# Macaron block on one core: how weight loads are cut, which engine adds the gate sums, where attention keeps its transposed tokens, and in what order blocks and attentions run

## The chip, the cores and the metric

The kernel runs on one core of a Trainium2 chip. The metric is device time in microseconds (us) for the whole program, lower is better; the time of a kernel is the median of its runs.

## The reference, cut to what matters

Eight sequences of 512 tokens with 512 features pass through a feed-forward part, an attention and a second feed-forward part, all in float32. The two feed-forward parts use the same weights.

```
x = x + 0.5 * ffn(layernorm(x), w_gate, w_up, w_down)
x = x + attn(layernorm(x), W_q, W_k, W_v, W_o)
x = x + 0.5 * ffn(layernorm(x), w_gate, w_up, w_down)

ffn:  h = silu(x @ w_gate) * (x @ w_up)            # hidden 2048
      keep, of each 4 neighbours in h, the 2 largest magnitudes
      return h @ w_down
attn: Q (16 heads of 32), K and V (4 heads, tiled), rotary positions on Q and K
      softmax(Q K^T / sqrt(32)) V, then @ W_o
```

## The kernel before, in words

**Blocks.** A block (b, i) is feed-forward part i (0 before, 1 after the attention) of sequence b: 16 blocks, run one after the other in the order of the list `blocks` (lines 90 to 93). Each block has four chunks of 512 hidden features, and each chunk two pairs. A pair is one Strassen-like product of seven half-size products (`woven`, lines 613 to 686), named by the quarter of the weight that they use: Q11, S1, S2, S4, S3, Q12, Q22 in this order. Their results are collected in `x`, `v` and `z` in PSUM and in `row` and `corner` in SBUF; VectorE (DVE) adds them (`add`, line 638), ScalarE copies or VectorE does (`copied`, lines 242 and 244). A product of eight matmul records of 256 columns takes 1.73 us of TensorE (PE). Then the two of four are kept by some 16 short VectorE instructions for each half of a chunk (`keep_two_of_four`, lines 393 to 452), while GpSimd (POOL) makes the sums `e` (lines 446 to 451). After every second chunk come seven products with `w_down` (`products`, line 532), whose results VectorE adds to the tokens (line 565).

**Gate sums.** S1 to S4 are sums of the quarters Q11, Q12, Q21, Q22 of the gate and up weights. The opening block (0, 0) loads four quarters of each pair and makes the sums of the pair after the current one when three groups of the current pair are through (`combine_gu`, line 688): VectorE adds (line 693, on the queue `for_later`, the last in rank), and SP stores each sum to DRAM (line 694). Every later block loads the sums (line 116). The sums for `w_down` are made in the opening block too: `combine_down` (line 492) loads a 1 MB chunk `raw` (line 496), GpSimd makes five sums of 1 x 512 per partition (line 505), and SP stores them (line 506); it runs for two chunks in each of two calls.

**Attention.** `attention(b)` (line 772) runs beside the blocks. It loads W_k, W_q, W_v into one tile (lines 775 to 778) and the rotary tables `cs` (line 780), then normalises and transposes the tokens (`layernorm_t`, line 278), projects, takes the maxima of the scores (VectorE, line 843), turns them into pieces in bfloat16 (lines 851 to 854), makes the exponentials (ScalarE, line 879), multiplies with V (line 887), sums the exponentials on VectorE (line 895), divides, and multiplies with W_o (line 972), which it loads as one DMA after the projections (line 830).

**Buffers.** The transposed tokens `xT` of blocks and of attentions come from the same pool of two (`xtp`, line 317); the list `in_xT` holds those in use, and the last step of a norm's scaling isn't passed while two are (line 349). The pool `p_slots` has two buffers of 8 KB per partition: `raw`, then in each attention `cs`, the first exponentials that become `total`, and the other exponentials `p`. PSUM has three single banks, taken in turn (`Bank`, line 225).

**Order of the work.** The program is written out by a planner in Python that keeps a clock for PE, VectorE and ScalarE. The main loop (line 1047) goes through the groups of the blocks; n counts groups, a half-size product of a pair counts 0.5, and a block is WIDTH = 42 units of n. After each group it may let each side stage (a norm for the next block, an attention, `combine_down`) take one step, if the step is due by n and what it waits for is ready by the planner's clock. A side has a first and a last n (lines 1003 to 1017) and its steps are spread between them in proportion to WEIGHTS; an attention has 57 steps with weights of 44.1 in all, the first 19 (norm and projections) at 0.5. Attention's stretch before is computed by lines 1007 to 1017: it starts no sooner than the last one ended, is moved to the start of a block if it would start more than 17 units into one, and gets an equal share of what is left or 1.4 blocks, whichever is longer. The norm for a block stands from 15 to 2 units ahead of it. VectorE's work waits in three queues (`urgent`, `put_off`, `for_later`) and in the steps of `keep_two_of_four`, and is written out when the planner's clock lets it fit (`fill`, line 374). All DMAs are issued by SP, in program order; a DMA that waits for its buffer or its source holds the ones behind it.

Of the kernel before, what the change touches and what calls it, by code (L numbers as in the profile page):

```python
# [11 lines left out]
FP = mybir.dt.float32  # L12
BF = mybir.dt.bfloat16
AF = mybir.ActivationFunctionType
ALU = mybir.AluOpType
# [11 lines left out]
def macaron_block(  # L27
# [59 lines left out]

    Q11, Q12, Q22, Q21, S1, S2, S3, S4 = range(8)
    gu_sums = [dram.tile([P, 4, 2, ND // 2, P], FP, name=f"gu_{i}") for i in range(2 * NCH)]
    blocks = [(0, 0), (1, 0)]  # L90
    for b in range(2, B):
        blocks += [(b, 0), (b - 2, 1)]
    blocks += [(B - 2, 1), (B - 1, 1)]
    coming = deque()
    for block in blocks:
        for i in range(2 * NCH):
# [181 lines left out]
    def layernorm_t(got, tag, src=None, xb=None):  # L278
# [33 lines left out]

        def turn(t):
            if t == 0:
                assert len(in_xT) < 2
                in_xT.append(got)
                got["xT"] = xtp.tile([P, ND, S], FP, tag="xT", name="xT")
            xT = got["xT"]
            tr = transposed([xn[t][:, c * P : (c + 1) * P] for c in range(ND)])
            nc.scalar.copy(xT[:, :, t * P : (t + 1) * P], tr.tile)  # L320
            tr.free(end=takes("act", 0.6, pe_heard()))
# [11 lines left out]
        if xb is None:  # L333
            there = at["pe"] + 10.0
            yield lambda: there
            found = [soon(0.9, partial(moments, t)) for t in (0, 1)]
            yield now
            found += [soon(0.9, partial(moments, t)) for t in (2, 3)]
            yield partial(when, found[:2])
            ensure(found[:2])  # L340
            scales((0, 1))
            yield partial(when, found)
            ensure(found)
            scales((2, 3))
            yield by_scalar
            for t in range(NT):
                normalise(t)
                end = at["act"]
                yield by_scalar if t < NT - 1 else lambda: max(end, by_scalar()) if len(in_xT) < 2 else None
            for t in range(NT):  # L350
                turn(t)
                yield by_scalar if t < NT - 1 else now
            if tag == "xf":
                sums()
        else:

            function(AF.Sqrt)
            for t in range(NT + 1):
                if t < NT:
                    moments(t)  # L360
                    va = rs[:, 0, t : t + 1]
                    nc.vector.tensor_scalar(va, mv[:, t, 1:2], EPS, None, ALU.add)
                    nc.scalar.activation(va, va, AF.Sqrt)
                if t:
                    i = t - 1
                    nc.vector.reciprocal(rs[:, 1, i : i + 1], rs[:, 0, i : i + 1])
                    nc.vector.tensor_scalar(
                        xn[i], xb[:, i, :], mv[:, i, 0:1], rs[:, 1, i : i + 1], ALU.subtract, ALU.mult
                    )
                    turn(i)  # L370
            function(AF.Silu)
            sums()
# [119 lines left out]
    def combine_down(g):  # L492

        for c in range(2 * g, 2 * g + 2):
            raw = p_slots.tile([P, 4, D], FP, "raw")
            nc.sync.dma_start(out=raw, in_=w_down[c])
            there = at["pe"] + 12.0
            yield lambda: there
            yield now
            quarter = {f"{i + 1}{j + 1}": raw[:, i::2, j * HD2 : (j + 1) * HD2] for i in range(2) for j in range(2)}  # L500
            sums = wa_slots.tile([P, 6, 2, HD2], FP, "sums")

            for i, name in enumerate(SUMS):
                op = ALU.add if name[2] == "+" else ALU.subtract
                nc.gpsimd.tensor_tensor(sums[:, i], quarter[name[:2]], quarter[name[3:]], op)
                nc.sync.dma_start(out=combined[g, name][:, c % 2 * 2 : c % 2 * 2 + 2, :], in_=sums[:, i])
            yield now
        done_down.add(g)
# [13 lines left out]
    def ffn(b, final, last):  # L522
# [165 lines left out]
        def combine_gu(i):  # L688

            w = [quarters[(b, final), i, q] for q in range(8)]  # L690

            def one(j, a, b, op):
                nc.vector.tensor_tensor(w[j], a, b, op)
                nc.sync.dma_start(out=gu_sums[i][:, j - S1], in_=w[j])

            gu_made[i] = [
                later(0.62, partial(one, j, w[a], w[b], op), at["pe"], for_later)
                for j, a, b, op in (
                    (S1, Q21, Q22, ALU.add),
                    (S2, S1, Q11, ALU.subtract),  # L700
                    (S3, Q11, Q21, ALU.subtract),
                    (S4, Q12, S2, ALU.subtract),
                )
            ]

        opens = (b, final) == blocks[0]
        hs, last_one = [], []
# [64 lines left out]
    def attention(b):  # L772
        ensure(written[b, 0])
        wa = wa_slots.tile([P, ND, D + 2 * KV], FP, "wqkv")
        for src, col in ((w_k, D), (w_q, 0), (w_v, D + KV)):
            nc.sync.dma_start(
                out=wa[:, :, col : col + src.shape[1]], in_=src.rearrange("(c p) n -> p c n", p=P)
            )
        cs = p_slots.tile([P, 4, S], FP, "cs")
        nc.sync.dma_start(out=cs[:, :2, :], in_=rope.rearrange("a p s -> p a s"))  # L780
        got = {}
        yield from layernorm_t(got, "xa", tokens[b][1])
        xT = got["xT"]
        qT = qkvp.tile([P, ND, S], FP, tag="qT", name="qT")
        kT = qkvp.tile([P, S], FP, tag="kT", name="kT")
# [2 lines left out]
        def projected(dst, col, scale):  # L788
# [13 lines left out]
            ps.free([read])  # L802
            soon(0.65, partial(nc.vector.scalar_tensor_tensor, sw, sw, scale, cs[:, 1, :], ALU.mult, ALU.mult))
            made = soon(0.65, partial(nc.vector.tensor_tensor, dst, dst, sw, ALU.add))
            return [p_slots.used(w_slots.used(made))]

        of_k = projected(kT, D, 1.0)
        yield now
# [14 lines left out]
                )  # L823
        multiplied(3.57)
        fill()
        in_xT.remove(got)
        nc.scalar.copy(v, vps.tile)
        vps.free(end=takes("act", 0.6, pe_heard()))
        wo = wa_slots.tile([P, ND, D + 2 * KV], FP, "wo")
        nc.sync.dma_start(out=wo[:, :, :D], in_=w_o.rearrange("(c p) n -> p c n", p=P))  # L830
        yield partial(when, of_k + of_q[0])

        def scores(c, t, nm):
# [86 lines left out]
        ensure(of_k + of_q[0])  # L920
        for t in range(NT):
            found = scores(0, t, nm)
            yield partial(when, found)
        pieces = in_pieces(nm)
        yield partial(when, pieces)
# [74 lines left out]
        return WIDTH * blocks.index((b, i))  # L1000


    sides = [(11, 18, 6, partial(combine_down, 0), None, None), (22, 32, 6, partial(combine_down, 1), None, None)]
    for b, i in blocks[1:]:
        stage = partial(layernorm_t, normed[b, i], "xf", tokens[b][2 * i])
        sides.append((place(b, i) - 15, place(b, i) - 2, NORM, stage, ("attention", b) if i else None, None))
    before = 0
    for b in range(B):

        left = place(B - 1, 1) - 13 - before  # L1010
        first = max(before, place(b, 0) + WIDTH + 16)
        if first % WIDTH > 17:
            first += WIDTH - first % WIDTH
        last = min(place(b, 1) - 13, max(before + left / (B - b), first + 1.4 * WIDTH))
        assert last - first > ATTENTION * 0.8
        sides.append((first, last, ATTENTION, partial(attention, b), ("attention", b - 1) if b else None, ("attention", b)))
        before = last
    sides.sort(key=lambda s: s[0])

    for _ in layernorm_t(normed[0, 0], "xf", xb=xs[0, 0]):  # L1020
# [98 lines left out]
```

## Time and profile before

| what | us |
|---|---|
| median of 3 runs (lowest, highest) | 3226.03 (3221.42, 3229.11) |
| the profiled execution's own time | 3222.35 |
| its span in the trace | 3220.5 |
| mean granted clock of PE | 0.999 |
| first matmul record, last product's end | 6.2, about 3216.5 |
| gate sums on VectorE (line 693), 32 instructions | 26.4 |
| `w_down` sums on GpSimd (line 505), 20 instructions | 27.3 |
| sums `e` and `h` on GpSimd (lines 446 to 451), 310 instructions | 424.8 |
| `w_q` and `w_o`, 1 MB each, issue to landing, median | 9.0, 5.2 |
| `raw`, 1 MB, issue to landing, median | 7.2 |

The span is the profiled execution from its first to its last instruction. A line of a stretch gives from:to, its length, and for each engine the busy time with the number of instructions (PE, PEld, the weight loads, DVE, ACT, POOL), then the granted clock of PE as a share, the busy share of the DMA engines and the GB/s. A line of the waits gives the waiting engine, tile and line, what it waited for, the time in total, the number of waits and the longest. A line of the timeline gives the start, the length, the engine, line and operation, the tile written and those read, the number of instructions merged, and in brackets the idle time before with what ended it.

### The profile page before, as it was taken

What the parts mean: (1) busy time and instruction counts of PE and PEld (TensorE: products, weight loads), DVE (VectorE), ACT (ScalarE), POOL (GpSimd) and SP (SyncE); (2) the same over time, 40 slices, a digit from 0 to 9 for tenths busy, and PEclk for the clock granted to TensorE, in tenths of its full rate; (3) what the DMA queues carried; (4) which work ended last, traced back from release to release, by engine and by line L of the source; (5) the groups of instructions that cost most, each with busy time, mean ns of one, the idle gap of its engine ahead of it and who ended that gap; (6) DMA issues with size and microseconds to landing.
All of it is one profiled execution on the core that took longest, in us unless ns stands there. A gap on an engine that the chain in (4) does not pass through costs nothing.

```text
span 3220.5 us, 43674 instructions
## 1 busy us (share of the span) xinstructions
PE 3180.1 (99%) x15880; PEld 2320.9 (72%) x15880; DVE 2281.7 (71%) x4869; ACT 1182.0 (37%) x1669; POOL 608.1 (19%) x888
## 2 busy tenths in 40 slices
PE   8999999999999999999999999999999999999999
PEld 6886668766776677767776668666776668666886
DVE  6867875678577775887578766678577775787554
ACT  2222552145324441354314532145324542255211
POOL 2422011211221112111121112111120122201120
PEclk9999999999999999999999999999999999999999
DMA  7762345433533434434543345333533446234451
GB/s 241 245 215 95 113 145 171 138 116 111 194 111 122 157 121 160 138 125 150 166 140 122 119 155 197 120 108 113 202 102 121 156 124 214 95 112 147 152 172 46
DMA packets 249285, 463.21 MB, mean 144 GB/s; under 512 B 24432, under 2 KB 64368, under 8 KB 248304
## 3 DMA queue, kind: packets, MB, share of 16 engines
q1 hardware_dynamic: 249072, 460.42, 43.3%
q8 instruction: 127, 2.08, 0.3%
q14 instruction: 86, 0.70, 0.1%
HBM read 421.53 MB, written 38.80 MB: 143 GB/s over the span
## 4 chain that ended last, share of the span: by engine, by line
PE 94%; DVE 3%; DMA 1%; ACT 1%; issue 0%; SPq 0%; DVEq 0%; ACTq 0%
PE x L624 26%; PE y L552 23%; PE v L624 13%; PE z L624 6%; PE proj L792 4%; PE sc L838 4%; PE st L871 4%; PE ops L887 4%; PE y L972 3%; PE tr L262 2%; PE gu L599 1%; PE den L903 1%; PE vps L817 1%; PE y L582 1%; PE st L876 1%; DMA xn<-x 1%
## 5 line engine op out<-in xcount | busy, mean ns | idle before, releaser
L624 PE MATMUL x<-ts,w 128*128 128x256 f32 x3000 | 720.2, 383 | 6.2 <-DVE corner L638 5.9
L624 PEld LDWEIGHTS x<-ts,w 128*128 128x128 f32 x3000 | 561.0, 190 | 151.4 <-issue 48.1
L552 PE MATMUL y<-wd,h 128*128 128x256 f32 x1984 | 455.2, 383 | 9.0 <-DVE h L440 6.4
L552 PEld LDWEIGHTS y<-wd,h 128*128 128x128 f32 x1984 | 372.8, 190 | 97.2 <-issue 28.8
L446 POOL TENSOR_TENSOR e<-h 128x512 f32<-128x512 f32 x62 | 96.6, 1559 | 1495.7 <-DVE h L440 1364.5
L164 DVE TENSOR_REDUCE nm<-sc 128x1 f32<-128x512 f32 x512 | 320.8, 683 | 63.5 <-PE sc L838 62.0
L565 DVE SCALAR_TENSOR_TENSOR x<-y,x 128x512 f32<-128x512 f32 x372 | 242.2, 686 | 135.6 <-PE y L552 133.8
L552 PE MATMUL y<-wd,e 128*128 128x256 f32 x1488 | 335.3, 380 | 1.0 <-PE den L903 1.0
L552 PEld LDWEIGHTS y<-wd,e 128*128 128x128 f32 x1488 | 281.3, 190 | 53.5 <-issue 11.0
L164 DVE TENSOR_TENSOR total<-total,p 128x512 f32<-128x512 f32 x384 | 266.2, 734 | 58.2 <-ACT p L879 58.2
L879 ACT ACTIVATE p<-st 128x2048 f32<-128x2048 f32 x96 | 179.6, 1870 | 283.2 <-PE st L876 191.3
L254 ACT ACT_TABLE_LOAD x206 | 264.3, 1283 | 4.4 <-PEq L1108 0.7
L673 ACT ACTIVATE h<-x 128x256 f32<-128x256 f32 x125 | 47.5, 380 | 592.8 <-PE x L624 573.1
L242 ACT COPY row<-x 128x512 f32<-128x512 f32 x210 | 122.9, 585 | 383.2 <-PE x L624 382.3
L624 PE MATMUL v<-ts,w 128*128 128x256 f32 x1000 | 238.8, 382 | 3.5 <-ACT xT L320 2.9
L624 PE MATMUL x<-xT,w 128*128 128x256 f32 x1000 | 239.8, 383 | 0.0
L624 PE MATMUL z<-xT,w 128*128 128x256 f32 x1000 | 239.4, 382 | 0.0
L624 PE MATMUL v<-xT,w 128*128 128x256 f32 x1000 | 239.0, 382 | 0.4 <-ACT corner L242 0.4
L624 PEld LDWEIGHTS x<-xT,w 128*128 128x128 f32 x1000 | 186.4, 190 | 50.8 <-issue 24.0
L624 PEld LDWEIGHTS v<-ts,w 128*128 128x128 f32 x1000 | 187.6, 190 | 46.9 <-issue 15.1
L624 PEld LDWEIGHTS z<-xT,w 128*128 128x128 f32 x1000 | 186.4, 190 | 48.2 <-issue 20.9
L624 PEld LDWEIGHTS v<-xT,w 128*128 128x128 f32 x1000 | 187.3, 190 | 45.5 <-issue 11.8
(109 smaller groups left out, 4114.0 us busy)
## 6 DMA issues: line engine op xcount, KB each, us to landing
w<-gu SPq DMA_DIRECT2D x472, 256.0 KB, 3.3
w<-in_w_gu SPq DMA_DIRECT2D x394, 256.0 KB, 3.3
wd<-wd SPq DMA_DIRECT2D x155, 512.0 KB, 3.8
wd<-in_w_down SPq DMA_DIRECT2D x124, 256.0 KB, 4.9
x<-x SPq DMA_DIRECT2D x64, 256.0 KB, 2.6
xn<-x SPq DMA_DIRECT2D x64, 256.0 KB, 6.9
x<-in_x SPq DMA_DIRECT2D x32, 256.0 KB, 3.4
gu<-w SPq DMA_DIRECT2D x32, 256.0 KB, 2.6
```

The lines of the kernel that those rows point to most:

```text
L164: self.does()
L242: nc.scalar.copy(dst, src)
L254: nc.scalar.activation(dummy[:, 1:2], dummy[:, 0:1], f)
L552: nc.tensor.matmul(out=y.tile[:, t, :], lhsT=part[:, t * P : (t + 1) * P], rhs=operands[i][:, n, :], start=(n == 0), stop=(n == 3),)
L565: nc.vector.scalar_tensor_tensor(to, y.tile, 0.5 * sign, to, ALU.mult, ALU.add)
L624: nc.tensor.matmul(out=bank.tile[:, m, :], lhsT=lhs[:, m, k, :], rhs=rhs[:, k, :], start=(first and m == 0 and k == 0), stop=(k == 1), ski ...
L792: nc.tensor.matmul(out=ps.tile, lhsT=wa[:, k, col : col + P], rhs=xT[:, k, :], start=(k == 0), stop=(k == ND - 1))
L838: nc.tensor.matmul(out=sc[:, kv, :], lhsT=qT[rows, c, t * P : (t + 1) * P], rhs=kT[rows, :], start=True, stop=True)
L871: nc.tensor.matmul(out=st[:, kv, :], lhsT=kT[rows, t * P : (t + 1) * P], rhs=qT[rows, c, :], start=True, stop=False)
L879: nc.scalar.activation(p, st, AF.Exp)
L887: nc.tensor.matmul(out=ops[rows, :], lhsT=v[:, t, rows], rhs=p[:, kv, :], start=(t == 0), stop=(t == NT - 1))
L972: nc.tensor.matmul(out=y.tile, lhsT=qT[:, k, t * P : (t + 1) * P], rhs=wo[:, k, :D], start=(k == 0), stop=(k == ND - 1))
```

## The change

Five things are done together.

1. The gate sums of the opening block are added by GpSimd, at the place where they were put on the queue before, and each is stored by SP right behind it.
2. Loads of 1 MB are cut into DMAs of 256 KB, each issued at a step of its side stage: `raw`, W_q, W_o; the rotary tables in two. In the attention the tokens are now loaded first, and W_k, W_v, the tables and W_q follow one at each of the first eight steps of the norm. `combine_down` has ten steps instead of six, and stretches from 10 to 19 and from 22 to 34.
3. Attention's `xT` is taken from `p_slots`; only the blocks' `xT` count in `in_xT`.
4. The order of blocks becomes, with b.i for block (b, i): 0.0, 1.0, 2.0, 3.0, 0.1, 4.0, 1.1, 2.1, 5.0, 6.0, 3.1, 7.0, 4.1, 5.1, 6.1, 7.1. Before it was 0.0, 1.0, 2.0, 0.1, 3.0, 1.1, 4.0, 2.1, 5.0, 3.1, 6.0, 4.1, 7.0, 5.1, 6.1, 7.1.
5. The attentions get equal stretches of n, one behind the other, from 58 to 617.

```diff
-    blocks = [(0, 0), (1, 0)]
-    for b in range(2, B):
-        blocks += [(b, 0), (b - 2, 1)]
-    blocks += [(B - 2, 1), (B - 1, 1)]
+    first_of = {0: 0, 1: 1, 2: 2, 3: 3, 5: 4, 8: 5, 9: 6, 11: 7}
+    second_of = {4: 0, 6: 1, 7: 2, 10: 3, 12: 4, 13: 5, 14: 6, 15: 7}
+    blocks = [(first_of[i], 0) if i in first_of else (second_of[i], 1) for i in range(2 * B)]
...
-                assert len(in_xT) < 2
-                in_xT.append(got)
-                got["xT"] = xtp.tile([P, ND, S], FP, tag="xT", name="xT")
+                if tag == "xf":
+                    assert len(in_xT) < 2
+                    in_xT.append(got)
+                    got["xT"] = xtp.tile([P, ND, S], FP, tag="xT", name="xT")
+                else:
+                    got["xT"] = p_slots.tile([P, ND, S], FP, "xT")
...
-            nc.sync.dma_start(out=raw, in_=w_down[c])
-            there = at["pe"] + 12.0
-            yield lambda: there
-            yield now
+            for r in range(4):
+                nc.sync.dma_start(out=raw[:, r], in_=w_down[c][:, r])
+                there = at["pe"] + 5.0
+                yield now if r < 3 else lambda: there
...
-            def one(j, a, b, op):
-                nc.vector.tensor_tensor(w[j], a, b, op)
+            for j, one, two, op in (
+                (S1, Q21, Q22, ALU.add),
+                (S2, S1, Q11, ALU.subtract),
+                (S3, Q11, Q21, ALU.subtract),
+                (S4, Q12, S2, ALU.subtract),
+            ):
+                nc.gpsimd.tensor_tensor(w[j], w[one], w[two], op)
                 nc.sync.dma_start(out=gu_sums[i][:, j - S1], in_=w[j])
-            gu_made[i] = [
-                later(0.62, partial(one, j, w[a], w[b], op), at["pe"], for_later)
...
-            ]
+            gu_made[i] = [Done(at["pe"] + 8.0)]
...
-        for src, col in ((w_k, D), (w_q, 0), (w_v, D + KV)):
-            nc.sync.dma_start(
-                out=wa[:, :, col : col + src.shape[1]], in_=src.rearrange("(c p) n -> p c n", p=P)
-            )
         cs = p_slots.tile([P, 4, S], FP, "cs")
-        nc.sync.dma_start(out=cs[:, :2, :], in_=rope.rearrange("a p s -> p a s"))
+        loads = deque()
+        for src, col in ((w_k, D), (w_v, D + KV)):
+            loads.append((wa[:, :, col : col + KV], src.rearrange("(c p) n -> p c n", p=P)))
+        for i in range(2):
+            loads.append((cs[:, i], rope[i]))
+        for k in range(ND):
+            loads.append((wa[:, k, :D], w_q[k * P : (k + 1) * P, :]))
         got = {}
-        yield from layernorm_t(got, "xa", tokens[b][1])
+        for ready in layernorm_t(got, "xa", tokens[b][1]):
+            if loads:
+                dst, src = loads.popleft()
+                nc.sync.dma_start(out=dst, in_=src)
+            yield ready
...
-        nc.sync.dma_start(out=wo[:, :, :D], in_=w_o.rearrange("(c p) n -> p c n", p=P))
...
         for t in range(NT):
             found = scores(0, t, nm)
+            nc.sync.dma_start(out=wo[:, t, :D], in_=w_o[t * P : (t + 1) * P, :])
...
-    sides = [(11, 18, 6, partial(combine_down, 0), None, None), (22, 32, 6, partial(combine_down, 1), None, None)]
+    sides = [(10, 19, 10, partial(combine_down, 0), None, None), (22, 34, 10, partial(combine_down, 1), None, None)]
...
-        left = place(B - 1, 1) - 13 - before
-        first = max(before, place(b, 0) + WIDTH + 16)
-        if first % WIDTH > 17:
-            first += WIDTH - first % WIDTH
-        last = min(place(b, 1) - 13, max(before + left / (B - b), first + 1.4 * WIDTH))
+    bounds = [WIDTH + 16 + b * (place(B - 1, 1) - 13 - WIDTH - 16) / B for b in range(B + 1)]
+    for b, (first, last) in enumerate(zip(bounds, bounds[1:])):
```

The smaller edits left out let a norm for an attention pass without counting in `in_xT` (line 349), and record the last use of `cs` one buffer back in `p_slots` (line 805).

## The prediction

> **What bounds the kernel now.** I read the page's busy line and chain first, then the table of stretches (where PE is idle), then the waits, then the timeline at the largest gaps.
>
> ```profile
> PE 3180.1 (99%) x15880; PEld 2320.9 (72%) x15880; DVE 2281.7 (71%) x4869; ACT 1182.0 (37%) x1669; POOL 608.1 (19%) x888
> ...
> PE 94%; DVE 3%; DMA 1%; ACT 1%; issue 0%; SPq 0%; DVEq 0%; ACTq 0%
> ```
>
> PE is the bound, and the diff leaves every matmul in place. So the whole prize is 3220.5 - 3180.1 = 40.4 us of PE idle, plus time at a lower clock. The stretches say where it lies: the second figure of each row, PE busy, is taken from the first, the length. The first row is the opening block; the others are the eight attentions, each from its first weight load to its last product.
>
> ```profile
> 26.00:134.00 108.00, 100.21 (x449) 85.28 (x448) 88.41 (x173) 26.25 (x44) 52.12 (x55) 0.98 0.72 249
> ...
> 206.60:504.00 297.40, 296.28 (x1527) 203.59 (x1526) 217.42 (x452) 124.25 (x169) 46.55 (x73) 1.00 0.42 139
> 549.20:862.00 312.80, 305.43 (x1568) 211.39 (x1567) 226.69 (x483) 120.88 (x161) 53.51 (x78) 1.00 0.41 136
> 862.90:1216.00 353.10, 352.61 (x1798) 253.86 (x1797) 259.09 (x551) 141.84 (x200) 68.40 (x107) 1.00 0.44 142
> 1216.80:1571.00 354.20, 353.71 (x1796) 254.97 (x1795) 258.26 (x549) 133.16 (x182) 68.01 (x107) 1.00 0.42 140
> 1595.80:1923.00 327.20, 325.45 (x1662) 229.54 (x1662) 245.40 (x523) 128.45 (x176) 60.32 (x82) 1.00 0.43 144
> 1992.90:2308.00 315.10, 307.05 (x1567) 212.48 (x1566) 226.73 (x483) 120.92 (x162) 53.22 (x78) 0.99 0.40 134
> 2307.40:2652.00 344.60, 343.90 (x1754) 245.63 (x1754) 257.54 (x546) 142.77 (x199) 66.21 (x105) 1.00 0.44 141
> 2701.80:2998.00 296.20, 295.46 (x1523) 202.84 (x1522) 216.71 (x451) 123.65 (x168) 46.51 (x73) 1.00 0.42 139
> ```
>
> Idle: opening 7.8 us; attentions 0 to 7: 1.1, 7.4, 0.5, 0.5, 1.8, 8.1, 0.7, 0.7 (20.7 together). The other 11.9 are the start (7.9 in the first 26 us) and the end (4.0 after 3200), which the change doesn't touch. Attentions 1 and 5 hold three quarters of the attentions' share.
>
> ```profile
> PE x L624 <- DVE corner L638: 5.9, 4, 4.7
> ...
> DVE w L693 <- DMA w<-in_w_gu: 9.9, 4, 4.0
> ```
> ```profile
> 60.35 4.92 DVE L693 TENSOR_TENSOR w<-w 128x512 f32<-128x512 f32 x3 [4.01 <-DMA w<-in_w_gu]
> ...
> 67.12 3.47 PE L624 MATMUL x<-ts,w 128*128 128x256 f32 x8 [4.70 <-DVE corner L638]
> ...
> 72.14 1.65 DVE L164 TENSOR_TENSOR h<-h,row 128x512 f32<-128x512 f32 x1
> 73.19 1.72 POOL L449 TENSOR_TENSOR e<-h 128x512 f32<-128x512 f32 x1
> ```
>
> The opening's largest gap is head-of-line blocking: a gate sum on DVE (L693) waits 4.01 us for its quarter, then is slow; the add of `corner` (L638) stands behind it, and PE waits 4.70 us for that add. In attentions 1 and 5 the same five gaps stand at the same places: 1.4 (PE on the maxima), 1.8 (on the pieces L854), 2.45 (on `h` L440), 1.45 (on xT at the block's start), 0.3. All are DVE or ACT a little late in a crowded stretch; no engine is full.
>
> **The Trainium skill.** "SBUF — State Buffer", Who interferes with whom: a DVE instruction with two SBUF inputs and a GpSimd one that reads SBUF exclude each other for a whole instruction. The trace agrees: the L164 multiply at 72.14 takes 1.65 us beside GpSimd, against 0.69 at 210.78. "GPSIMD Engine Reference", 3.1: an add is 1.96 times slower there; here the same shape takes 1.27 us (L505 median) against 0.69 (L693 median), 1.85 times. "TensorE: Matmul & The Clock Gate", What's actually happening: after idling the clock is halved. The trace shows it: eight matmuls at 67.12 took 3.47 us, the next eight at 70.42 took 1.89; in attention 5 the chain has 11.69 us for 44 matmuls after the 2.45 us gap, 10.00 elsewhere. Attention 1's equal gap was not followed by it, so it is not certain.
>
> **Part 1, gate sums to GpSimd.** Removed from DVE in 26 to 134 us: 24 instructions, 21.2 us busy, and 10.1 us idle ahead of them. Added to GpSimd: 24 at 1.27 (30.5 us) to 1.72 (contended; 41 us), on top of 52.1 busy of 108. GpSimd becomes 76 to 86% busy. Each long GpSimd instruction costs DVE something: DVE instructions in this stretch sum to about 16 us more than their quiet durations beside 32 long GpSimd ones, 0.5 each. 24 more cost DVE 12 us, at 1.0 each 24, still below the 31 removed. The DMA wait now blocks GpSimd's queue, where only the chunk sums (L505), `e` (L446 to L451) and the next norm's scales stand behind it, none needed within a few us; behind the waiting sum on SP stand its store and the next quarters (rival D). So the 4.70 gap, its half-clock (3.47 - 1.89 = 1.6) and the 0.34 at 81.29 go: 6.6. New is a wait for S4: chunk 1's sums end at 64.7 (57.67 + 7.05), four sums later it is 69.8; without its 6.3 us delay the next pair would start at 64.1 and want S4 three products of 1.73 later, at 69.3. Late by 0.5, with the signal 0.6. The three other gaps (0.56, 1.55, 0.62: `h` and a down weight) stay, as the masking on DVE still meets GpSimd. Gain 6.0; bounds: all 9.4 (7.8 + 1.6), or the loss in rival D.
>
> **Part 2, loads in 256 KB parts.** Chunks of `w_down` no longer stand as 1 MB ahead of gate quarters (one was issued at 50.55, the four quarters at 51.28). This is part of why the sum waited; the gain is in part 1. In the attention the `xn` loads now precede the weights (`xn<-x` lands in a median 6.9 us, `x<-x` in 2.6); PE lost 0.63 us to that in attention 0 (220 us), counted below. 68 more issues at about 0.5 us are 34 us of SP's queue in 3220: in the opening 12, in each attention 7, behind gate loads that wait for PE anyway (SP waited 734 us on PE at L116 alone). The second chunk pair now ends at 34 units instead of 32; its sums are first loaded in the next block, past 42. I take nothing; without that cover, 3.5 us would fall on one attention's quarters.
>
> **Part 3, order and equal shares.** One unit is a 3.46 us group. A block is 42. From lines 1007 to 1017, the attentions before had 55, 59, 72, 72, 65, 59, 69 and 69 units, starting 16, 0, 17, 5, 0, 0, 17 and 2 into a block. After, each has (617 - 58)/8 = 69.9, starting 16, 2, 30, 16, 2, 29, 15 and 1 in. Attentions 6 and 7 before had the new width at two of the new phases, with 0.7 us idle each; 0.7 is the value for an attention after. Attention 1: 7.4 to 0.7, 6.7. Attention 5: 8.1 to 0.7 and its half-clock 11.69 - 10.00 = 1.7, together 9.0. Attentions 0 and 4: 0.4 and 1.1. Attentions 2, 3, 6, 7: -0.4. Sum 16.8.
>
> Against that, attentions 2 and 5 start 30 units in. At 69.9/44.1 = 1.585 units per weight their turns fall 36 to 39 units in, the next block's at 36 to 40. No attention before did that. Two turns in one pass need two banks of three while `x` and `v` hold two: the second waits for ScalarE's 0.58 us copy (L320) and two signals, about 0.95. Bounds: 0, and 7.4 each (the worst attention seen). I take two such waits and 0.6 at the boundary, 2.5 each: -5.0. Gain of the part 11.8.
>
> **Part 4, xT in a `p` buffer.** No instruction is added. The buffer is the one of the former attention's exponentials, last read before its output products, so nothing waits. It frees the two `xT` buffers for the blocks; without it the overlap above would hold a norm back. Price 0.
>
> **Sum.** 6.0 + 11.8 = 17.8. The profiled execution took 3222.35 (span 3220.5 and 1.85 around it): 3204.6. The median of the runs stands 3.7 higher, at 3226.03: 3208.
>
> **Rivals.** A (forecast, 0.50): 3208, own range 3203 to 3213. B (0.21): the overlap and the opening cost nothing: 9.4 + 16.8 = 26.2, 3200. For it: DVE at 73% in attentions. C (0.17): attentions 2 and 5 cost 7.4 each, 9.8 more: 3218. For it: two norms and the projections at once. D (0.08), slower: SP issues the next quarters only behind the stores of four GpSimd sums. The loop is 4 x 1.72 + 1.88 (four issues) + landing 7.25 (seen at 53.01) = 16.0 us against a pair's 12.1, six times 3.9, plus two chunk sums of 7.05 in the way: 37.5 us of new idle in place of 6.6, 30.9 worse, less 11.8: 3245. It decides once the loop passes 12.1; with medians (5.1 + 1.9 + 3.3 = 10.3) it doesn't. E (0.04): the gaps come of the phase (0 to 2), not of the width, and return three times at 6.7: 3228. Against it: attentions 4 and 7 before, at 0 and 2, lost 1.8 and 0.7.
>
> **Numbers.** 0.2% (6.5 us) is about what a measurement can tell from no change. Faster: A, B and half of C, 0.80. Same: 0.11 (C's other part, most of E). Slower: 0.09 (D). The range runs from B less the runs' spread, 3196, to C plus it, 3221.
>
> **What would show it.** Right: no gap over 1 us between 55 and 80 us and no DVE wait on `w`; attention 1 and 5 under 2 us idle; no half-clock after the start. Wrong: PE waiting on GpSimd's `w` in the opening (D); PE waiting on `tr` copies or xT at the boundaries of attentions 2 and 5 (C); gaps on L440 or L854 at phase 2 (E).

## The result, and the profile after

The changed kernel is slower by 17.5 us. Its median is 3242.93 us (six runs, 3242.06 to 3243.84) against 3225.46 us for the kernel before (six runs, 3221.42 to 3229.11): a ratio of 1.0054, interval 1.0041 to 1.0067. The forecast was 3208 us. The profiled execution took 3242.93 us with a span of 3241.1.

The busy line and the shares of the chain come first, as before the change.

```profile
PE 3186.3 (98%) x15880; PEld 2324.7 (72%) x15880; DVE 2308.4 (71%) x4848; ACT 1191.6 (37%) x1678; POOL 651.0 (20%) x920
...
PE 94%; DVE 4%; ACT 1%; DMA 0%; issue 0%; SPq 0%; DVEq 0%
```

PE still bounds the kernel, with the same 15880 matmuls; its idle time rose from 40.4 us to 54.8 (3241.1 - 3186.3), and its busy time by 6.2, since more of the same work ran at half clock. Two cells surprise. POOL took over 32 sums and rose by 42.9 us. DVE gave up 26.4 us of gate sums and is still 26.7 us busier. Some of that lies in the attentions, where the adds of `total` rose from 266.2 to 282.2 us; the opening is looked at first.

The table of stretches follows, cut again into the opening and the attentions, of which it shows 1, 2 and 5 (from:to, length, busy time of PE, PEld, DVE, ACT and POOL with instructions, clock, DMA share, GB/s).

```profile
26.00:160.00 134.00, 106.47 (x451) 89.55 (x450) 99.18 (x149) 26.12 (x44) 86.25 (x83) 0.91 0.61 207
...
579.50:928.00 348.50, 345.40 (x1748) 246.49 (x1747) 253.20 (x521) 135.29 (x186) 61.83 (x96) 1.00 0.43 142
928.80:1275.00 346.20, 344.18 (x1757) 245.93 (x1756) 253.06 (x540) 134.39 (x184) 63.33 (x93) 1.00 0.41 135
...
1971.50:2323.00 351.50, 347.63 (x1765) 248.54 (x1764) 256.55 (x543) 134.55 (x185) 68.97 (x106) 1.00 0.41 133
```

The opening now has 27.5 us of PE idle (7.8 before, in a stretch that was shorter) at a clock of 0.91. The attentions have 0, 3.1, 2.0, 1.0, 2.6, 3.9, 1.4 and 1.5, together 15.4 where 20.7 stood. A cleaner cut is by blocks: from the first product of pair 1 of the opening block to the first product of the next block it took 121.4 us before and takes 146.9 after. From there to the last product it took 3067.4 and takes 3062.2. **The change loses 25.5 us in the opening block and gains 5.1 in all the rest.** (These are the two profiled executions, whose spans differ by 20.6 us; the medians differ by 17.5.)

PE's waits between 26 and 160 us and the timeline of PE say what the opening waits for.

```profile
PE x L630 <- DVE corner L644: 14.0, 3, 6.8
PE y L558 <- DMA wd<-wd: 6.5, 1, 6.5
PE z L630 <- DVE row L644: 5.1, 1, 5.1
```
```profile
57.59 3.48 PE L630 MATMUL x<-ts,w 128*128 128x256 f32 x8 [6.84 <-DVE corner L644]
...
127.23 6.20 PE L558 MATMUL y<-wd,e 128*128 128x256 f32 x16 [6.50 <-DMA wd<-wd]
```

The one gap of 4.70 us behind `corner` has become four gaps of 5 to 7 us: these two, one of 6.57 ahead of 78.01 and one of 5.08 ahead of 156.61. Three stand behind adds of VectorE and one behind a down weight. The eight matmuls behind each of the three take 3.47 to 3.52 us where 1.89 is usual, and the sixteen behind the down weight 6.20 where 3.62 is usual: the half clock, now four times.

VectorE no longer waits for a quarter. What it does ahead of the first gap, and what GpSimd does at that time, stand in the timelines of the two engines:

```profile
44.34 1.76 DVE L422 TENSOR_TENSOR m<-a 128x512 bf16<-128x512 f32 x1
...
48.83 1.36 DVE L429 TENSOR_TENSOR m<-m 128x256 bf16<-128x256 bf16 x1
...
52.65 0.28 DVE L433 TENSOR_TENSOR m<-m 128x256 bf16<-128x256 bf16 x1
...
56.86 0.68 DVE L644 TENSOR_TENSOR corner<-x,corner 128x512 f32<-128x512 f32 x1
```
```profile
43.83 7.48 POOL L511 TENSOR_TENSOR sums<-raw 128x512 f32<-128x512 f32 x5 [7.05 <-DMA w<-in_w_gu]
51.27 5.52 POOL L704 TENSOR_TENSOR w<-w 128x512 f32<-128x512 f32 x4
```

Five chunk sums and four gate sums run on GpSimd without a pause for 13 us. Beside them the same masking steps of VectorE that take 0.68, 0.41 and 0.28 us in a quiet moment take 1.76, 1.49 and 1.36 (the one at 52.65 began just between two of GpSimd's sums and took its quiet 0.28). Nine such steps between 44.34 and 56.94, lines 422 to 441, are together 9.0 us above their quiet durations, and `corner` stands behind them in VectorE's order. That makes the theory: **GpSimd's sums exclude VectorE's two-input steps, and they do it where VectorE has a row of short steps ahead of an add that PE needs.** The rival is D of the prediction: SP's queue stands behind GpSimd's stores, and PE waits for loads. SP's waits between 26 and 160 us make it worth testing:

```profile
SPq L705 <- POOL w L704: 41.6, 23, 7.6
SPq L512 <- POOL sums L511: 38.9, 20, 8.0
```

### The profile page after: what moved, and what is told of

Its sections match the earlier page's. It is cut to its first block, busy times and chain, and to the rows that moved or that the text cites. A ratio compares the mean times of both kernels' runs of the same rounds, so it can differ in the third digit from the quotient of the medians.

```text
span 3241.1 us, 43752 instructions
## 1 busy us (share of the span) xinstructions
PE 3186.3 (98%) x15880; PEld 2324.7 (72%) x15880; DVE 2308.4 (71%) x4848; ACT 1191.6 (37%) x1678; POOL 651.0 (20%) x920
## 4 chain that ended last, share of the span: by engine, by line
PE 94%; DVE 4%; ACT 1%; DMA 0%; issue 0%; SPq 0%; DVEq 0%
PE x L630 26%; PE y L558 23%; PE v L630 13%; PE z L630 6%; PE proj L800 4%; PE st L877 4%; PE sc L844 4%; PE ops L893 4%; PE y L979 3%; PE tr L263 1%; PE gu L605 1%; PE den L909 1%; PE vps L825 1%; PE st L882 1%; PE y L588 1%; DVE total L165 1%
## 5 line engine op out<-in xcount | busy, mean ns | idle before, releaser
L165 DVE TENSOR_TENSOR total<-total,p 128x512 f32<-128x512 f32 x384 | 282.2, 773 | 45.6 <-ACT p L885 45.6
L630 PEld LDWEIGHTS v<-ts,w 128*128 128x128 f32 x1000 | 187.0, 190 | 49.6 <-issue 17.4
```

Source lines behind the costliest of these rows:

```text
L165: self.does()
L630: nc.tensor.matmul(out=bank.tile[:, m, :], lhsT=lhs[:, m, k, :], rhs=rhs[:, k, :], start=(first and m == 0 and k == 0), stop=(k == 1), ski ...
```

## The experiments

Medians are in us; "before" is the kernel before, measured beside each group of experiments, at 3224.9 to 3225.3 each time. An interval is that of the ratio to it.

### The gate sums alone

The changed kernel with the gate sums back on VectorE:

```diff
-                nc.gpsimd.tensor_tensor(w[j], w[one], w[two], op)
-                nc.sync.dma_start(out=gu_sums[i][:, j - S1], in_=w[j])
-            gu_made[i] = [Done(at["pe"] + 8.0)]
+            gu_made[i] = [later(0.62, partial(one, j, w[a], w[b], op), at["pe"], for_later) ...]
```

> The changed kernel with the gate sums back on VectorE, all else of the change kept. Theory 1 (GpSimd and VectorE exclude each other in SBUF: GpSimd's sums stretch VectorE's short masking steps, and the adds that PE waits for stand behind them) and theory 2 (SP's queue stands behind GpSimd's sums, so quarters and down weights come late) both expect the opening block to fall from 175 us to about 150 at the first product of the second block, and the time from 3242.9 to about 3218. Theory 3 (the cut loads and later chunk sums of combine_down did it) expects 3236 to 3243.

Measured: 3225.08, ratio 1.0002 (0.9994 to 1.0011). The opening block takes 129.5 us instead of 146.9, and the rest 3060.6 instead of 3062.2. So of the 25.5 us, 17.4 belong to the gate sums on GpSimd. The other 8.1 remain, and with them the time stays 7 us above what I had expected here.

The kernel before with the gate sums on GpSimd, and nothing else:

```diff
-            gu_made[i] = [later(0.62, partial(one, j, w[a], w[b], op), at["pe"], for_later) ...]
+                nc.gpsimd.tensor_tensor(w[j], w[one], w[two], op)
+                nc.sync.dma_start(out=gu_sums[i][:, j - S1], in_=w[j])
+            gu_made[i] = [Done(at["pe"] + 8.0)]
```

> The kernel before with the gate sums moved to GpSimd, nothing else. Theories 1 and 2: most of the 25 us lost in the opening come with this part alone, 3225.5 + 15 to 25 = 3240 to 3250. Theory 3: at most 5 us, 3226 to 3231, since the loads are those of before.

Measured: 3250.69, ratio 1.0082 (1.0067 to 1.0097). By itself the move costs 25.8 us, more than in the whole change. The opening block takes 149.8, with gaps of 6.04, 3.91, 15.17 (a down weight) and 3.05 us. The other parts are not needed for the loss.

### Exclusion, or only a busy GpSimd

The changed kernel with each gate sum replaced by a sum of 2 columns and two fills of the same tile. GpSimd stays busy, 1.3 us for each sum, and its stores stay where they were, but the fills only write. This kernel leaves out the gate sums.

```diff
-                nc.gpsimd.tensor_tensor(w[j], w[one], w[two], op)
+                nc.gpsimd.tensor_tensor(w[j][:, 0, 0, :2], w[one][:, 0, 0, :2], w[two][:, 0, 0, :2], op)
+                for part in range(2):
+                    nc.gpsimd.memset(w[j], 0.01)
```

> The changed kernel with each gate sum on GpSimd replaced by a sum of two columns (which keeps the wait for its quarters) and two fills of the whole tile, which read nothing: left out are the gate sums themselves. GpSimd is about as long at work at each sum (some 1.1 to 1.5 us), and SP's queue and the program order are those of the changed kernel. Theory 1 (exclusion needs GpSimd's reads of SBUF): VectorE's short steps beside the gate sums fall back from 1.35 to 0.28 us, the gaps of 6.8 and 6.6 us shrink below 3 us each, time 3220 to 3232. Theory 2: the gaps stay, 3240 to 3246.

Measured: 3232.10, ratio 1.0022 (1.0013 to 1.0031), 10.8 us below the changed kernel. Of the two gaps behind `corner`, the first shrinks from 6.84 us to 0.81 and the second, 6.57, is gone; the last two go from 1.85 and 5.08 to 1.33 and 1.13. New are two waits of PE on GpSimd's `w`, 1.50 and 0.68. Timelines of GpSimd and of VectorE:

```profile
49.50 1.11 POOL L706 MEMSET w<- 128x512 f32 x2
...
50.94 1.11 POOL L706 MEMSET w<- 128x512 f32 x2
```
```profile
47.90 1.48 DVE L424 TENSOR_TENSOR m<-a 128x256 bf16<-128x256 f32 x1
...
49.64 0.28 DVE L429 TENSOR_TENSOR m<-m 128x256 bf16<-128x256 bf16 x1
```

At 47.90 a chunk sum still reads beside the step; from 49.06 on there are fills, and the steps fall to 0.28 though GpSimd is as busy. That is the exclusion itself. (The second gap is weaker evidence: here the masking ahead of it falls mostly into a pause of GpSimd, from 56.0 to 61.6.) But one gap grew, that for the down weight:

```profile
121.94 6.32 PE L558 MATMUL y<-wd,e 128*128 128x256 f32 x16 [13.18 <-DMA wd<-wd]
```

So a second cause stands beside the first, and it doesn't need the gate sums' reads.

### SP's queue behind GpSimd

First, the stores of the gate sums are issued behind the next pair's quarter loads instead of ahead of them, which is the loop of rival D cut open:

```diff
-                nc.sync.dma_start(out=gu_sums[i][:, j - S1], in_=w[j])
+                stores.append(partial(nc.sync.dma_start, out=gu_sums[i][:, j - S1], in_=w[j]))
...
                         load_quarters(*[key for key in quarters if key[:2] == ((b, final), i)])
+                        while stores:
+                            stores.pop(0)()
```

> The changed kernel with the stores of the gate sums put on SP's queue behind the next pair's quarter loads instead of right behind the sums. Theory 2: the quarters no longer wait for GpSimd, the gaps of 6.8 and 6.6 us go, 3225 to 3230. Theory 1: both gaps stay within 2 us of what they were, 3238 to 3246.

Measured: 3241.68, ratio 1.0054 (1.0038 to 1.0071), 1.3 us below the changed kernel, which is within the spread of the runs. The gaps at `corner` become 5.26 and 5.07: the loop is worth some 1.5 us in each, and the rest of them stays. A second wait for a down weight, 1.97 us, takes part of that back. So rival D's loop through the quarters is not what costs the time; that its total, 3245, came close is luck.

Second, the stores of the chunk sums, in the second call of `combine_down`, come one step later:

```diff
                 nc.gpsimd.tensor_tensor(sums[:, i], quarter[name[:2]], quarter[name[3:]], op)
+            if g:
+                made = at["pe"] + 12.0
+                yield lambda: made
+            for i, name in enumerate(SUMS):
                 nc.sync.dma_start(...)
...
-    ... (22, 34, 10, partial(combine_down, 1), None, None)]
+    ... (22, 34, 12, partial(combine_down, 1), None, None)]
```

> The changed kernel with the stores of the sums of chunks 2 and 3 (combine_down's second call) one step later in SP's queue than the sums, so that SP doesn't stand behind GpSimd there while PE needs the next down weight. If SP's place behind the chunk sums made the gap of 6.5 us at 121 us (PE on the down weight), that gap falls below 2 us and with the half-clock after it the time falls by 5 to 9 us, to 3234 to 3238; the gaps of 6.8 and 6.6 us at 51 and 71 stay. If the load was late for another reason (the DMA engines are full), the gap stays, 3241 to 3245.

Measured: 3234.50, ratio 1.0031 (1.0019 to 1.0043), 8.4 us below the changed kernel. The opening block takes 139.7 us instead of 146.9. SP's own queue shows the order in the changed kernel and then in this one:

```profile
112.28 5.70 SPq L512 DMA_DIRECT2D wd<-sums  x5
...
120.47 0.38 SPq L519 DMA_DIRECT2D wd<-wd  x1
```
```profile
110.25 0.33 SPq L523 DMA_DIRECT2D wd<-wd  x1
...
117.58 3.29 SPq L516 DMA_DIRECT2D wd<-sums  x5
```

In the changed kernel the load of the down weight is issued at 120.47, when five stores have waited for GpSimd's sums one after the other; with the stores later, it is issued at 110.25. PE's wait for it falls from 6.50 us to 0.19. The gaps behind `corner` (6.54, 6.58) stay, as expected of the first cause; the wait for `row` near the block's end grows from 5.08 us to 8.38, and the gap of 1.85 us ahead of it is gone. The wait for the down weight belongs to part 1 too: with the gate sums back on VectorE, PE doesn't wait for a down weight at all, and with the gate sums alone on GpSimd it waits 15.17 us. The two removals, 10.8 and 8.4, add up to more than the 17.9 that the gate sums cost; both at once were not run.

### What is left: the cut loads of the opening, and the attentions

The changed kernel with the opening of the kernel before: gate sums on VectorE, `raw` as one DMA of 1 MB, the old stretches of `combine_down`. All edits to the attentions, the order and the shares stay.

```diff
-            for r in range(4):
-                nc.sync.dma_start(out=raw[:, r], in_=w_down[c][:, r]) ...
+            nc.sync.dma_start(out=raw, in_=w_down[c]) ...
...
-    sides = [(10, 19, 10, partial(combine_down, 0), None, None), (22, 34, 10, ...
+    sides = [(11, 18, 6, partial(combine_down, 0), None, None), (22, 32, 6, ...
```

> The changed kernel with the opening block of before: gate sums on VectorE, raw in one DMA of 1 MB, combine_down with its old steps and window. Kept: order, equal shares, xT in p, the attention's loads in parts. If part 3 is worth what the trace of the changed kernel says (from the second block's start to the end 3060.6 us with the sums on VectorE, against 3067.3 before, 6.7 less), it takes 3225 - 6.7 = 3218, the opening 121 to 123 us. Against e1 (3225.1) the difference is then the price of the cut raw loads and their later chunk sums, about 7. If those cost nothing, it stays at 3223 to 3227.

Measured: 3219.17, ratio 0.9981 (0.9973 to 0.9990). Against the kernel with only the gate sums put back (3225.08) that is 5.9 us less, and the opening block takes 122.6 instead of 129.5. So `raw` in four parts and the stretched steps cost 5.9 to 6.9 us; they weren't tried apart. In that kernel the first chunk's five sums start at 45.33 and the next at 63.92, where this one has the first at 35.44 and the next at 58.31; a part goes out at each step, so the last is later than the whole was. The gap of 2.69 us that PE had there ahead of 54.70 is gone here.

Against the kernel before, this one gains 6.1 us. Next, the order and the shares alone, on the kernel before:

```diff
-    blocks = [(0, 0), (1, 0)] ...
+    first_of = {0: 0, 1: 1, 2: 2, 3: 3, 5: 4, 8: 5, 9: 6, 11: 7} ...
...
-        first = max(before, place(b, 0) + WIDTH + 16) ...
+    bounds = [WIDTH + 16 + b * (place(B - 1, 1) - 13 - WIDTH - 16) / B for b in range(B + 1)]
```

> The kernel before with the new order of blocks and the equal shares alone; attention's xT in the old pool of two, loads as before. If the xT buffer and the attention's loads are worth nothing (as forecast), it equals e5, 3218, within 2 us. If the xT buffer matters, the norms of the blocks behind attentions 2 and 5 are held back and PE waits there: 3225 to 3240.

Measured: 3230.95, ratio 1.0017 (1.0010 to 1.0025): by themselves they cost 5.7 us (order and shares weren't tried apart). That is in the range that I had expected if `xT` matters. The missing 11.8 us must come from the attentions' loads or from `xT`. Two runs divide these. The kernel with the old opening and the attentions' loads whole and ahead of the tokens again:

```diff
+        for src, col in ((w_k, D), (w_q, 0), (w_v, D + KV)):
+            nc.sync.dma_start(
+                out=wa[:, :, col : col + src.shape[1]], in_=src.rearrange("(c p) n -> p c n", p=P)
+            )
         cs = p_slots.tile([P, 4, S], FP, "cs")
-        loads = deque() ...
+        nc.sync.dma_start(out=cs[:, :2, :], in_=rope.rearrange("a p s -> p a s"))
...
```

> e5 with the attention's loads as before: W_k, W_q, W_v and the tables whole and ahead of the tokens, W_o in one DMA. xT stays in p. If the whole loads make e7's gaps (the down weights stand behind 2.5 MB on the rings), they return: 3228 to 3232. If the xT buffers do, this equals e5 within 3 us.

Measured: 3231.94, ratio 1.0022 (1.0013 to 1.0031). And the same old opening, with attention's `xT` back in its pool of two:

```diff
-                    got["xT"] = p_slots.tile([P, ND, S], FP, "xT")
+                assert len(in_xT) < 2
+                in_xT.append(got)
+                got["xT"] = xtp.tile([P, ND, S], FP, tag="xT", name="xT")
...
+        in_xT.remove(got)
         nc.scalar.copy(v, vps.tile)
```

> e5 (3219.2) with attention's xT back in the old pool of two, counted in in_xT as before. If the gaps of 4.7 and 4.5 us that order and shares alone (e7) have at the start of attentions 2 and 5 come of the attention's whole loads, this kernel equals e5 within 3 us. If they come of the two xT buffers, they return here: 3228 to 3232.

Measured: 3216.99, ratio 0.9978 (0.9968 to 0.9987), in the spread of the kernel it was made from (3215.57 to 3221.81). So `xT` is worth nothing that these runs can tell, with whole loads (3230.95 and 3231.94) as with parts, and the changed loads are worth 12.8 us (3231.94 - 3219.17) with the new order. These loads are cut and also issued later, and these two things weren't tried apart. The queue of SP at the start of attention 2 says how; first with the order alone, then with the loads in parts.

```profile
902.15 0.50 SPq L777 DMA_DIRECT2D wqkv<-in_w_q  x1
...
903.93 3.31 SPq L287 DMA_DIRECT2D xn<-x  x4
907.36 2.94 SPq L514 DMA_DIRECT2D wd<-wd  x2
```
```profile
902.86 1.80 SPq L287 DMA_DIRECT2D xn<-x  x4
...
905.90 3.77 SPq L519 DMA_DIRECT2D wd<-wd  x2
```

The new order starts attentions 2 and 5 thirty units into a block, just where the block issues its down weights. With whole loads, W_k, W_q, W_v, the tables and the tokens are issued ahead of `wd`, and its two halves land after 8.2 us (median); with parts, the tokens and W_k are, and they land after 5.0. PE shows the price, in the timeline of the kernel with the order alone; the kernel with parts has no such gap.

```profile
916.36 9.18 PE L553 MATMUL y<-wd,h 128*128 128x256 f32 x32 [4.73 <-DMA wd<-wd]
```

Such waits come to 9.9 us in that kernel and 11.3 with whole loads, against 1.0 with parts. Half clock adds to it: the 32 matmuls behind this gap take 9.18 us, and 7.14 in the opening block of the kernel with parts. So the parts pay for where the new order starts two of the attentions; with the old order they weren't tried alone.

### The same exclusion inside the attentions

In attentions 1, 4 and 5 a gap of 1.85 to 1.95 us stands at the same place. The timelines of PE, VectorE and GpSimd of the changed kernel, in attention 1:

```profile
711.97 1.53 PE L877 MATMUL st<-qT,kT 32*128 32x512 f32 x8 [1.85 <-DVE nm L165]
```
```profile
701.59 6.13 DVE L165 TENSOR_TENSOR total<-total,p 128x512 f32<-128x512 f32 x4
...
708.85 1.87 DVE L165 TENSOR_REDUCE nm<-sc 128x1 f32<-128x512 f32 x3
```
```profile
702.10 1.71 POOL L455 TENSOR_TENSOR e<-h 128x512 f32<-128x512 f32 x1
703.78 1.72 POOL L456 TENSOR_TENSOR h<-h 128x512 f32<-128x512 f32 x1
```

Four adds of `total` take 6.13 us, 1.53 each, beside GpSimd's sums; behind them the reductions for the maxima come 0.62 apart, and PE's `st` waits for the last of the maxima. Over the whole kernel the new order puts more of these adds beside GpSimd's sums: their mean was 734 ns before and is 775 with order and shares alone. The kernel with the old opening, in which those sums (lines 452 to 457) only write:

```diff
-                    nc.gpsimd.tensor_tensor(sums[:, 2], h11, h12, ALU.add)   # and the four others
+                    nc.gpsimd.tensor_tensor(to[:, 0, :2], one[:, 0, :2], two[:, 0, :2], ALU.add)
+                    for part in range(2):
+                        nc.gpsimd.memset(to, 0.01)
```

> e5 with GpSimd's sums e and h of every chunk replaced by sums of two columns and two fills of the same tiles: left out are these sums. GpSimd stays as long at work but hardly reads SBUF. If the exclusion of GpSimd and VectorE also makes the gaps in the attentions (1.85 us at 710 and 2177, 1.95 at 1814 in the changed kernel, where four total adds took 6.1 us), these gaps and the half-clock after them go: 8 to 14 us under e5, VectorE's mean for a total add falls from 0.77 to 0.69 us. If the gaps come of the crowded stretch itself, they stay, and it is within 3 us of e5.

Measured: 3209.08, ratio 0.9951 (0.9938 to 0.9965), 10.1 us below the kernel it was made from. This kernel leaves out the sums `e` and `h`. In the profiled executions 10.7 us are gained behind the opening block (3049.8 against 3060.5) and 2.8 lost in it. The group of the `total` adds, before, with reading sums and with writing ones:

```profile
L164 DVE TENSOR_TENSOR total<-total,p 128x512 f32<-128x512 f32 x384 | 266.2, 734 | 58.2 <-ACT p L879 58.2
```
```profile
L165 DVE TENSOR_TENSOR total<-total,p 128x512 f32<-128x512 f32 x384 | 282.3, 773 | 45.6 <-ACT p L889 45.6
```
```profile
L165 DVE TENSOR_TENSOR total<-total,p 128x512 f32<-128x512 f32 x384 | 247.6, 684 | 49.1 <-ACT p L891 49.1
```

A mean of 773 ns falls to 684, and the three gaps of 1.9 us go. That these sums read thus costs this kernel about 10 us as they are placed, and a better placing of them can hardly bring more.

### A version that follows from this

The old opening again, but chunks 0 and 1 are loaded right behind the first eight quarters, in parts of 256 KB, and their sums are made at once, while nothing is masked yet:

```diff
+    early = []
+    for c in range(2):
+        early.append(p_slots.tile([P, 4, D], FP, "raw"))
+        for r in range(4):
+            nc.sync.dma_start(out=early[c][:, r], in_=w_down[c][:, r])
...
-    sides = [(11, 18, 6, partial(combine_down, 0), None, None), ...
+    sides = [(8, 12, 4, partial(combine_down, 0), None, None), ...
```

> e5 with chunks 0 and 1 of w_down loaded right behind the first eight quarters, in parts of 256 KB, and their sums on GpSimd when VectorE has no masking yet (before 43 us). If the opening's gap of 4.7 us with its half-clock comes of the 1 MB load ahead of the quarters and of chunk 1's sums beside the gate sums, it goes: 5 to 7 us under e5, about 3212. If the early 2 MB delay the quarters of the third pair instead, PE waits at 29 to 45 us and it is 3218 to 3225.

Measured: 3213.86, ratio 0.9966 (0.9953 to 0.9978). It is faster than both kernels, 5.3 us below the one it was made from. The sums of chunk 0 start at 15.49 and those of chunk 1 at 29.62, both ahead of the first masking, and the opening block takes 118.7 us; its gaps over 1 us are 1.85, 1.38, 1.55 and 1.42.

Last, that kernel with the planner's clock for VectorE set forward for the exclusion:

```diff
                     nc.gpsimd.tensor_tensor(sums[:, 2], h11, h12, ALU.add)
+                    takes("dve", 0.6)
...
                     nc.gpsimd.tensor_tensor(h21, h21, h11, ALU.subtract)
+                    takes("dve", 2.4)
```

> e10 (3213.9) with the planner's clock of VectorE put forward where it writes out GpSimd's sums of a chunk: 0.6 us at the first half, 2.4 at the second (four total adds beside them took 6.1 us instead of about 2.6). If PE waits because the planner takes a maximum or an add for done too early, the gaps of 1.85 to 1.95 us in attentions 1, 4 and 5 shrink, since PE is given other work first: 3207 to 3212. If VectorE is short of time there whatever the order, it stays at 3213 to 3216.

Measured: 3214.04, ratio 0.9969 (0.9958 to 0.9980): no gain in all. From the second block on it takes 3055.8 us instead of 3060.6, and attentions 1, 4 and 5 fall from 3.1, 2.6 and 3.9 us idle to 1.3, 0.7 and 2.3. The opening block loses that again (125.1 instead of 118.7), in a new gap of 6.41 us at 89 us. Telling the planner only outside the opening wasn't tried.

## Why the prediction was wrong

**The failed step** is in part 1: "Each long GpSimd instruction costs DVE something ... 24 more cost DVE 12 us, at 1.0 each 24, still below the 31 removed." The size held, at its upper end. In the opening block VectorE is busy 97.0 us before and 95.4 with the gate sums alone on GpSimd, though 21.2 us of its own work are gone: the 24 sums cost it 19.6 us, 0.8 each. With the rest of the change in place it is 104.6 with the gate sums, 23.7 us of them, and 106.0 without: 1.0 each. The comparison was the error: it set a sum against a sum, and 10.1 of the 31 were time in which VectorE only waited. The exclusion isn't spread; nine masking steps lose 9.0 us in one place, on an engine that works in order, with PE's add behind them. And the move freed nothing: VectorE's busy time is 2309.0 us with the gate sums on it and everything else changed, and 2308.4 without them. The forecast gain of 6.0 became a loss of 17.9, or 25.8 when done alone. Of the marks that I had set, no gap over 1 us between 55 and 80 us, two of 6.8 and 6.6 stand there; what I hadn't listed as a mark was that the add could be late with no wait on `w` at all.

**The queue of SP** is the second step that failed. "None needed within a few us" was said of what stands behind GpSimd's own queue; of SP's queue part 1 named a gate sum's store and the next quarters, rival D's loop. The loop is worth about 1.3 us. What counted was a third thing behind the stores, a down weight: 6.5 us of gap and some time at half clock, 8.4 by experiment. I hadn't looked for everything else that SP issues there.

**Part 2** was priced at nothing, and that was wrong twice with opposite signs: 5.9 lost in the opening, as later parts make later sums; 12.8 gained in the attentions, as less stands ahead of the down weights. The opening's reason is read from the timelines, not shown by a run of its own.

**Part 3** was mis-sized: with the attentions' loads in parts the rest gained 5.1 us where I took 11.8, and by itself it lost 5.7. The five old gaps of attentions 1 and 5 did go, 7.4 to 3.1 and 8.1 to 3.9, but others came. The term is "0.7 is the value for an attention after". Attentions 2 and 5 came out at 2.0 and 3.9, 5.9 together against 6.4 forecast (0.7 and 2.5 each). That this is close is half luck, since 1.85 us of it is the exclusion's gap in attention 5; the rest is of the kind that was forecast. In attention 2 two norms transpose at once and the second `xT` comes late:

```profile
959.15 1.99 PE L630 MATMUL x<-xT,w 128*128 128x256 f32 x8 [0.90 <-ACT xT L324]
```

The other six have 9.6 us in place of 4.2. Crowding alone wasn't the cause of the gaps that are left; the largest, in attentions 1, 4 and 5, came of the exclusion, which equal shares don't remove. Forecast half clocks didn't go either: one of 3.41 us follows the gap in attention 1, another the one in attention 5. That the new order loses time without the loads in parts is a dependence that I didn't see.

**Part 4** was right: 0 was taken, and no difference shows. Its worry was not: with the old pool of two nothing is slower (3216.99), and the waits on `xT` of 0.90 and 0.73 us in attentions 2 and 5 aren't there.

The sum, part by part in the prediction's terms, by the runs: 17.9 lost to part 1 (3242.93 - 3225.08, the late down weight in it), 5.9 to the cut loads of the opening, and 6.1 gained by order, shares and attention's loads together. Net 17.7, of 17.5 measured. These are the steps of one chain of kernels, so that they add up proves nothing; taken in another order they would be sized differently, as the 25.8 of the first part alone shows.

**The Trainium skill.** "SBUF — State Buffer", Who interferes with whom, says that VectorE with two SBUF inputs contends with a GpSimd instruction that reads SBUF and not with one that only writes. The runs agree: a masking step takes 1.35 us beside sums and 0.28 beside fills, and a reduction for the maxima, which has one input, takes 0.68 in the changed kernel beside a sum or not. I had cited it and then averaged it. "DMA: Bandwidth & Descriptors", Bandwidth, advises to batch DMAs to 1 MiB or more for bandwidth. It doesn't settle this case: cutting and spreading attention's loads gained 12.8 us. Over an attention the DMA share is 0.41 to 0.44, but at the start of attention 2, from 906 to 912 us, the DMA engines are full either way, 1.03 with whole loads and the order alone and 1.02 with parts. What differs is what stands ahead of the down weight.

## What to carry to other kernels

Moving an elementwise sum from VectorE to GpSimd isn't a question of which engine has room: it is paid where the sum meets a row of two-input VectorE steps with something that the bounding engine needs behind them, so look at what stands at that time before summing busy shares. A store of a slow engine's result holds everything issued behind it on the same DMA-issuing engine; list all of it, and try the store behind the next load that has a due time. Load early what the slow engine needs, so that it works while the other one is idle.

## What the runs showed of the hardware

The half clock keeps to a grid. By the traces' own record of the granted clock, in all 14 kernels of this case every period of half clock between 26 us and the last product begins on a grid of the kernel's own in steps of 3.413 us, and lasts one to five whole steps. In the changed kernel the first four begin at 53.82, 74.30, 125.50 and 156.22 us, 6, 15 and 9 steps apart.

What decides is how long PE stood idle within one step, by its matmul records. In the same stretch, from full clock, a step with up to 1.72 us idle was never followed by half clock and one with more than 2.01 us always was; in between both happen. So the place of a gap counts beside its length. In the changed kernel the gap of 1.85 us ahead of 711.97 lies within one step and was followed by 3.41 us at half clock from 712.59. In the version with the early chunks the same gap ahead of 684.91 falls into two steps, 1.02 and 0.83 us, and was followed by none. This also answers what the prediction left open about the two gaps of 2.45 us before: in attention 1 it was split into 1.11 and 1.34 us, in attention 5 a step held 2.01.

"TensorE: Matmul & The Clock Gate", What's actually happening, ties the half clock to an idle window of about 3.4 us. The length agrees; that the window must be idle throughout does not, so here the measurement decides. A gap of about 2 us can cost up to half of 3.41, 1.7 us, on top, or nothing.

The exclusion lengthens both sides. In the changed kernel a GpSimd sum of 128x512 takes 1.27 us alone and 1.71 beside VectorE's adds, and those take 1.53 instead of 0.69.
